# One order for all five queues of a transformer block, planned while it is traced

## The chip, the cores and the metric

The kernel runs on one core of a Trainium2 chip. The metric is the device time of one execution in microseconds; beside it there is the profile of one execution of the same program. The engines are called as in the profile: PE is TensorE (matrix products), PEld its weight loads, DVE is VectorE, ACT is ScalarE, POOL is GpSimd, and SP is the queue from which this kernel issues all its DMAs.

## The reference, cut to what matters

The input x has 8 batches of 1024 tokens with 512 features. After one layer norm, causal attention with 16 heads of 32 features and a feed-forward network with blockwise FP4 quantisation run side by side on the same normalised tokens, and both are added to x:

```python
xn = _layernorm(x, axis=-1)
x = x + _L0_attn_ref(xn, W_attn, b_attn, W_proj, b_proj) + _L0_ffn_ref(xn, w_gate, w_up, w_down)

def fp4_quant_dequant(x):           # along the last dim, blocks of 16
    scale = jnp.maximum(jnp.max(jnp.abs(xb), axis=-1, keepdims=True) / 6.0, 1e-12)
    xn = xb / scale
    idx = jnp.searchsorted(_MID, jnp.abs(xn))
    return _GRID[idx] * jnp.sign(xn) * scale

gate, y = fp4_linear(x, w_gate), fp4_linear(x, w_up)      # 512 -> 1408
h = jax.nn.silu(gate) * y
return fp4_linear(h, w_down)                              # 1408 -> 512
```

`fp4_linear` quantises both its operands, so the weights, the normalised tokens and the hidden values all go through the quantisation. Everything is in float32.

## The kernel before

**Tiles and units.** Tokens are worked on in 64 tiles of 128 (`Tile`, eight to a batch). Attention is worked on in 64 units (`Unit`): two heads of one batch over its 1024 tokens. Values that are needed later (q and k split into a high and a low part, v, quantised tokens, attention outputs, partial results) go to DRAM and come back.

**The pieces of work**, each a generator that traces instructions and yields a cost in microseconds of PE time:

- `prepare` (with `normed`, `keep_quantised`, `project`): a tile's layer norm (L265 to L269: statistics on DVE, one power on POOL, one scaling on DVE), its transposes on PE with a copy by ACT (L222, L223), its quantised form, and, for each second tile, the q, k and v projections (L322, L359). ACT moves q and k from PSUM to the one buffer `full` (L333), DVE splits them (L342, L343), SP stores them.
- `maxima`: for a unit, all scores are computed once (L414) for their row maxima: DVE adds the causal mask in PSUM (L422) and takes the maximum (L423), then makes a small table of statistics that PE transposes (L437), ACT copies (L439, `statT`) and SP sends through DRAM into `shT`.
- `weigh`: scores are computed a second time with the maxima subtracted by an extra matmul (L497, L500), ACT takes the exponential (L508), POOL zeroes the masked part (L511) and adds up the sums (L469, L472), PE multiplies by v (L479) and sums the sums (L537).
- `network`: gate and up products of a tile in pairs of column chunks (L611), silu by ACT (L623), product by DVE (L626), quantisation, transposes, the down product (L596), and a part result (L603) kept in DRAM.
- `finish`: the attention output of a tile is loaded (`yT`, L677), normalised by the inverse sums (L687, L688), projected (L696) and added to the part result (L701).
- `weights_quantised`: 34 pieces of the three FFN weight matrices are loaded, quantised and transposed into SBUF; the first half beside the first batch's `prepare`, the second half over the first eight units.
- `quantised`: the quantisation, ten instructions of DVE (L201 to L215). For weight pieces the two multiplies by a spread scale (L208, L215) run on POOL.

**What sets the order.** The outer loop runs over the units. In step n it merges the preparation of tile n+10, the finish of tile n-10, `weigh` of unit n, the network's next tile (from n = 8 on; before that weights and `prepare_late`), and `maxima` of unit n+1. `merge` always advances the stream with the smallest share of its total done. `passed` advances one clock by the cost said, and actions that were put off with `Later` (mostly DMA issues) are traced when the clock passes their time. PE, ACT and SP keep the order in which the instructions were traced (`manual_schedule`); the order on DVE and POOL is chosen by the framework's scheduler when the program is built.

**PSUM.** The pool `ps_g` has six banks used in turn under the name `g`; `y` and `acc` have one bank each.

## Time and profile before

| | |
|---|---|
| time, median of 3 runs | 4896.89 us (4888.65 to 4902.39) |
| the profiled execution's own time | 4902.55 us |
| span of its instructions | 4900.8 us |
| mean granted TensorE clock | 0.957 |
| busy PE / DVE / POOL / ACT | 91% / 62% / 37% / 29% |
| mean DMA rate over the span | 123 GB/s of HBM |

The span runs from the first to the last instruction of one execution. Lines such as L423 are lines of the kernel's source. A PE time is modelled at its end, so a busy PE is not PE at its peak. A float32 matmul appears as two records in the profile. "A <- B" in a list of waits says that B's end released A; the columns after it are the total in us, how often, and the longest.

### The profile page before, as it was taken

What the parts mean: (1) busy time and instruction counts of PE and PEld (TensorE: products, weight loads), DVE (VectorE), ACT (ScalarE), POOL (GpSimd) and SP (SyncE); (2) the same over time, 40 slices, a digit from 0 to 9 for tenths busy, and PEclk for the clock granted to TensorE, in tenths of its full rate; (3) what the DMA queues carried; (4) which work ended last, traced back from release to release, by engine and by line L of the source; (5) the groups of instructions that cost most, each with busy time, mean ns of one, the idle gap of its engine ahead of it and who ended that gap; (6) DMA issues with size and microseconds to landing.
All of it is one profiled execution on the core that took longest, in us unless ns stands there. A gap on an engine that the chain in (4) does not pass through costs nothing.

```text
span 4900.8 us, 59197 instructions
## 1 busy us (share of the span) xinstructions
PE 4482.6 (91%) x18708; PEld 2698.6 (55%) x18708; DVE 3060.8 (62%) x6903; ACT 1444.1 (29%) x2892; POOL 1836.1 (37%) x2652
## 2 busy tenths in 40 slices
PE   6567778999999999999999999999999999999999
PEld 5444445555555555555555555555555555555554
DVE  6577665656566665656666565666666566666555
ACT  1122223332323333332333333233233333333210
POOL 2145443433433343333343334334333334444300
PEclk9778889999999999999999999999999999999999
DMA  6544443444544453554445445444445444333221
GB/s 189 165 111 120 121 119 90 139 118 131 151 120 136 132 145 115 136 147 124 132 134 141 118 141 143 124 136 132 135 125 141 138 124 114 95 90 77 67 64 63
DMA packets 609145, 605.35 MB, mean 124 GB/s; under 512 B 133824, under 2 KB 464064, under 8 KB 608832
## 3 DMA queue, kind: packets, MB, share of 16 engines
q1 hardware_dynamic: 608832, 601.57, 43.9%
q8 instruction: 149, 2.44, 0.2%
q14 instruction: 164, 1.34, 0.1%
HBM read 431.50 MB, written 169.87 MB: 123 GB/s over the span
## 4 chain that ended last, share of the span: by engine, by line
PE 68%; DVE 16%; ACT 2%; DMA 2%; issue 2%; POOL 1%; SPq 1%; ACTq 0%; DVEq 0%; POOLq 0%
PE g L611 23%; PE acc L596 9%; PE g L322 7%; PE y L479 5%; PE g L696 4%; PE g L497 4%; PE g L414 4%; PE g L359 4%; PE g L500 4%; DVE neg L423 3%; PE g L222 2%; DVE scale L201 1%; PE g L537 1%; DVE inv L204 1%; DVE g L422 1%
## 5 line engine op out<-in xcount | busy, mean ns | idle before, releaser
L472 POOL TENSOR_TENSOR sum<-sum,pr 128x512 f32<-128x512 f32 (+3 forms) x1024 | 948.4, 935 | 605.8 <-ACT pr L508 560.7
L508 ACT ACTIVATE pr<-g 128x512 f32<-128x512 f32 (+3 forms) x1536 | 680.2, 494 | 1280.5 <-PE g L500 1265.5
L423 DVE TENSOR_REDUCE neg<-g 128x1 f32<-128x512 f32 (+3 forms) x1536 | 811.5, 548 | 79.3 <-PE g L414 69.1
L511 POOL TENSOR_SCALAR_AFFINE_SELECT pr<-pr 128x128 f32<-128x128 f32 x1024 | 361.6, 358 | 1136.7 <-ACT pr L508 1111.5
L414 PE MATMUL g<-ks,qs 128*128 128x512 f32 (+3 forms) x1536 | 694.6, 499 | 88.6 <-ACT full L333 43.6
L611 PE MATMUL g<-wuT,xqT_in 128*128 128x512 f32 (+1 forms) x1536 | 707.8, 591 | 47.7 <-DVE neg L423 47.7
L497 PE MATMUL g<-shT,pick 128*128 128x512 f32 (+3 forms) x1536 | 646.3, 429 | 83.6 <-DVE neg L423 64.9
L611 PE MATMUL g<-wgT,xqT_in 128*128 128x512 f32 (+1 forms) x1536 | 678.9, 568 | 1.7
L596 PE MATMUL acc<-wdT,hqT 128*128 128x512 f32 x1408 | 667.4, 595 | 1.4 <-ACT hqT L223 1.4
L422 DVE TENSOR_TENSOR g<-g,mask 128x128 f32<-128x128 f32 x1024 | 286.8, 291 | 557.8 <-PE g L414 555.0
L322 PE MATMUL g<-xnT,wa 128*128 128x256 f32 x2048 | 504.4, 403 | 42.4 <-ACT xnT L223 26.1
L500 PE MATMUL g<-qs,ks 128*128 128x512 f32 (+3 forms) x1536 | 534.0, 355 | 0.0
L469 POOL TENSOR_TENSOR sum<-pr 128x512 f32<-128x512 f32 x256 | 339.7, 1339 | 485.7 <-ACT pr L508 475.7
L322 PEld LDWEIGHTS g<-xnT,wa 128*128 128x128 f32 x2048 | 417.7, 206 | 120.1 <-ACT xnT L223 27.6
L414 PEld LDWEIGHTS g<-ks,qs 128*128 128x128 f32 x1536 | 285.4, 197 | 319.8 <-issue 114.7
L611 PEld LDWEIGHTS g<-wuT,xqT_in 128*128 128x128 f32 x1536 | 286.5, 196 | 316.1 <-issue 201.7
L479 PE MATMUL y<-pr,vs 128*32 128x512 f32 (+3 forms) x3072 | 431.2, 516 | 24.1 <-POOL pr L511 23.3
L497 PEld LDWEIGHTS g<-shT,pick 128*128 128x128 f32 x1536 | 298.9, 195 | 244.9 <-DVE neg L423 109.1
L611 PEld LDWEIGHTS g<-wgT,xqT_in 128*128 128x128 f32 x1536 | 280.8, 191 | 234.5 <-issue 169.4
L596 PEld LDWEIGHTS acc<-wdT,hqT 128*128 128x128 f32 x1408 | 259.6, 190 | 230.5 <-issue 209.9
L500 PEld LDWEIGHTS g<-qs,ks 128*128 128x128 f32 x1536 | 300.8, 196 | 76.7 <-issue 45.0
L333 ACT ACTIVATE full<-g,bqk 128x256 f32<-128x256 f32 x256 | 107.3, 470 | 626.0 <-PE g L322 307.7
(98 smaller groups left out, 4740.7 us busy)
## 6 DMA issues: line engine op xcount, KB each, us to landing
wa<-in_L_attn_W_attn_dram SPq DMA_DIRECT2D x192, 512.0 KB
qs<-qk_kept SPq DMA_DIRECT2D x512, 128.0 KB
ks<-qk_kept SPq DMA_DIRECT2D x512, 128.0 KB
wp<-in_L_attn_W_proj_dram SPq DMA_DIRECT2D x93, 512.0 KB
qk_kept<-high SPq DMA_DIRECT2D x128, 256.0 KB
qk_kept<-full SPq DMA_DIRECT2D x128, 256.0 KB
y_kept<-yu SPq DMA_DIRECT2D x256, 128.0 KB
yT<-y_kept SPq DMA_DIRECT2D x128, 256.0 KB
```

The costliest lines, as they stand in the source:

```text
L322: nc.tensor.matmul(pq[:, j, :], lhsT=wa[:, c, j * P : (j + 1) * P], rhs=xnT[:, c, :], start=(c == 0), stop=(c == NC - 1),)
L414: nc.tensor.matmul(sc[:, :n], lhsT=un.qs[Q][:, r, i * P : (i + 1) * P], rhs=un.ks[h][:, r, :n], start=True, stop=True,)
L423: nc.vector.tensor_reduce(neg[:, Q + h, k : k + 1], sc[:, :n], AX.X, ALU.max, negate=True)
L469: nc.gpsimd.tensor_tensor(sums[r], prs[0][0], prs[1][0], ALU.add)
L472: nc.gpsimd.tensor_tensor(sums[r][:, q0:], sums[r][:, q0:], pr[:, q0:], ALU.add)
L479: nc.tensor.matmul(y[row : row + HD, q0:], lhsT=un.vs[h][:, jj, r * HD : (r + 1) * HD], rhs=pr[:, q0:], start=(j < 2), stop=(j >= last - 1 ...
L497: nc.tensor.matmul(w[:, q0:], lhsT=pick[:, Q * HU + r, :], rhs=un.shT[:, q0:], start=True, stop=False)
L500: nc.tensor.matmul(w[:, q0:], lhsT=un.ks[h][:, r, jj * P : (jj + 1) * P], rhs=un.qs[Q][:, r, q0:], start=False, stop=True,)
L508: nc.scalar.activation(pr[:, q0:], w[:, q0:], AF.Exp)
L511: nc.gpsimd.affine_select(out=pr[:, q0 : q0 + P], in_=pr[:, q0 : q0 + P], compare_op=ALU.is_ge, fill=0.0, base=0, pattern=[[1, P]], channe ...
L596: nc.tensor.matmul(tl.acc, lhsT=job.hqT[:, j, :], rhs=wdT[:, i, :], start=(i == 0), stop=(i == NI - 1))
L611: nc.tensor.matmul(job.g[:, : job.w], lhsT=job.tl.xqT[:, c, :], rhs=wT[:, c, job.i0 : job.i0 + job.w], start=(c == 0), stop=(c == NC - 1),)
```

## The change

The kernel now keeps a clock for each engine besides the one for PE, and every piece of work says to them what it puts on ACT, DVE and POOL. A step yields up to four values: its PE cost, the time from which its inputs should be there, how many free PSUM banks it needs, and its weight in the sharing. `merge` takes, among the streams whose share is within 0.3 of the smallest, one that can start now; if none can, it lets the clock pass to the earliest. `passed` handles put-off actions in the order of their times. All five engines are in `manual_schedule`, so DVE and POOL too keep the traced order.

The six banks become six fixed tiles (`Banks`); a step takes the one that the clock says is free first. The quantisation becomes the class `Quantised`: seven steps, each put off to its own time, spaced at 1.4 times their length; at most two are under way, with two `step` buffers where there was one. Only the first 17 weight pieces use POOL for the multiplies. The layer norm yields between the power on POOL and the scaling on DVE. The split of q and k, the load of the part result and the inverse of the sums have times of their own; `yu` has one buffer where it had two.

The diff, cut to its core:

```diff
+    def on(engine, us, after=0.0):
+        free[engine] = max(free[engine], clock[0], after + HOP) + us
+        return free[engine]
+
+    def act(columns, after=0.0, function="other"):
+        ...
+        return on("act", 0.1 + 0.00095 * columns + switch, after)
...
     def passed(us):
-        clock[0] += us
-        for entry in [e for e in waiting_list if e.due <= clock[0]]:
-            waiting_list.remove(entry)
-            entry.now()
+        end = clock[0] + us
+        while True:
+            due = [e for e in waiting_list if e.due <= end]
+            if not due:
+                break
+            first = min(due, key=lambda e: e.due)
+            waiting_list.remove(first)
+            clock[0] = max(clock[0], first.due)
+            first.now()
+        clock[0] = end
+
+    class Banks:
+        def __init__(self):
+            self.tiles = [ps_g.tile([P, W], F32, name=f"bank{k}") for k in range(6)]
+            self.at = [0.0] * 6
+        def when(self, count):
+            return sorted(self.at)[count - 1] if count else 0.0
+        def take(self):
+            k = self.at.index(min(self.at))
+            self.at[k] = float("inf")
+            return k, self.tiles[k]
+        def back(self, k, time):
+            self.at[k] = time
...
-    def quantised(src, w, xs, spreader=None):
...
+    class Quantised:
+        def __init__(self, src, w, xs, after=0.0, helper=False):
+            while len(running) > 1:
+                running[0].done()
+            running.append(self)
+            ...
+            start = max(0.0, after - clock[0])
+            for wide, us, engine, action in self.operations(src, w, xs, helper):
+                us = us + wide * w / CW
+                self.left.append(Later(start, lambda us=us, engine=engine, action=action: self.one(us, engine, action)))
+                start += SPREAD * us
+            self.expected = clock[0] + start
...
-            done.append((piece, quantised(raw, piece[4], raw, nc.gpsimd)))
-            yield 0.0
...
+            done.append((piece, Quantised(raw, piece[4], raw, helper=k < EARLY)))
+            while len(done) > (1 if k + 1 < len(pieces) else 0):
+                (_, dst, r, c, w), wq = done.pop(0)
+                yield 0.0, wq.ready(), 1
+                transposed(dst[:, c // P : (c + w) // P, r : r + P], wq.done(), w // P)
+                if len(pieces) > k + 2:
+                    loaded.append(load(*pieces[k + 2]))
+                yield 0.11 * w / P, 0.0, 0, 0.5
...
         nc.gpsimd.tensor_tensor(rstd, rstd, power, ALU.pow)
+        yield 0.0, pool(0.6, dve(1.05)), 0
         nc.vector.tensor_scalar(xt, xt, mv[:, 0:1], rstd, ALU.subtract, ALU.mult)
+        tl.ready = dve(0.6)
...
-                nc.vector.tensor_copy(high, full)
-                nc.vector.tensor_tensor(low, full, high.bitcast(F32), ALU.subtract)
+                def split(full=full, high=high, low=low):
+                    nc.vector.tensor_copy(high, full)
+                    nc.vector.tensor_tensor(low, full, high.bitcast(F32), ALU.subtract)
+                    dve(1.1)
...
-                stored.append(Later(4.0, store))
-                yield 3.4
+                stored.append(Later(end - clock[0] - 0.3, split))
+                stored.append(Later(end - clock[0] + 2.0, store))
+                yield 3.44, 0.0, 1
...
                     nc.vector.tensor_reduce(neg[:, Q + h, k : k + 1], sc[:, :n], AX.X, ALU.max, negate=True)
-                    yield n * 0.00044
+                    end = dve(0.08 + 0.00105 * n, end)
+                    banks.back(bank, end)
+                    yield cost, 0.0, 1
...
                 if j % 2 == 0 and waiting:
-                    yield weighted()
+                    yield 2 * cost, max(ready, emptied), 0
+                    yield weighted(), 0.0, 2
                     waiting = []
...
-            yu = p2.tile([P, W], F32, name="yu")
+            yu = p1.tile([P, W], F32, name="yu")
...
+        part = load_part() if tl.part is not None else None
+        yield 0.0, clock[0] + 6.0, 0, 1.0
         nc.vector.tensor_tensor(yT, yT, more, ALU.add)
         nc.vector.tensor_tensor(yT, yT, inv, ALU.mult)
-        yield 3.0
-        part = load_part() if tl.part is not None else None
+        yield 0.0, dve(1.4), 1, 1.0
...
+    def merge(streams):
+        live = [Stream(total, steps) for total, steps in ((t, s) for s, t in streams)]
+        while live:
+            least = min(s.share() for s in live)
+            start = lambda s: max(s.ready, banks.when(s.banks))
+            near = [s for s in live if s.share() - least < AHEAD_OF_OTHERS] or live
+            now = [s for s in near if start(s) <= clock[0] + 0.05]
+            if now:
+                s = min(now, key=Stream.share)
+            else:
+                s = min(near, key=start)
+                ...
+                if start(s) > clock[0]:
+                    passed(start(s) - clock[0])
+            if not s.step():
+                live.remove(s)
...
-        engines={mybir.EngineType.PE, mybir.EngineType.Activation, mybir.EngineType.SP}
+        engines={
+            mybir.EngineType.PE,
+            mybir.EngineType.Activation,
+            mybir.EngineType.DVE,
+            mybir.EngineType.Pool,
+            mybir.EngineType.SP,
+        }
...
-                streams.append((maxima(units[n + 1]), 7.0))
+                streams.append((maxima(units[n + 1]), 6.0))
```

## The prediction

> **What bounds the kernel now.** I read the page first (engines, slices), then the busy table by stage, then the waits of TensorE in each stage, then one stall in the timeline. From the page:
>
> ```profile
> PE 4482.6 (91%) x18708; PEld 2698.6 (55%) x18708; DVE 3060.8 (62%) x6903; ACT 1444.1 (29%) x2892; POOL 1836.1 (37%) x2652
> PE   6567778999999999999999999999999999999999
> PEclk9778889999999999999999999999999999999999
> ```
>
> TensorE is the bound from slice 8 on. Before that neither it nor any other engine is full, and its granted clock is low. The transpose of the 64 units' statistics (statT, one per unit) marks the stages: units' statistics start at 229.1 us, the feed-forward network joins at about 737, token preparation ends at about 4030, the last unit's statistics are at 4553.3. The busy table over these stretches (columns: stretch, length, then busy us of PE, weight load, DVE, ACT, POOL; clock; DMA share; GB/s):
>
> ```profile
> 0.00:229.00 229.00, 148.77 (x617) 121.39 (x617) 137.04 (x316) 37.74 (x79) 50.39 (x64) 0.85 0.60 183
> 229.00:737.00 508.00, 344.37 (x1590) 223.42 (x1590) 341.22 (x762) 135.64 (x303) 243.71 (x339) 0.83 0.43 117
> 737.00:4030.00 3293.00, 3146.05 (x13287) 1893.23 (x13286) 2059.08 (x4702) 1043.34 (x2070) 1257.06 (x1839) 0.97 0.47 132
> 4030.00:4553.00 523.00, 505.69 (x2129) 280.55 (x2128) 340.81 (x759) 174.86 (x341) 238.96 (x350) 0.99 0.37 92
> 4553.00:4901.00 348.00, 337.69 (x1095) 179.99 (x1091) 182.68 (x365) 52.52 (x99) 45.97 (x62) 1.00 0.21 65
> ```
>
> TensorE stands idle for 80, 164, 147, 17 and 10 us: 418 us in all, which is what there is to win, and the cycles lost to a low clock after a stall. What ended the idle time, for TensorE in the second stage and then in the third:
>
> ```profile
> PE g L437 <- DVE stat L433: 44.3, 9, 10.1
> PE g L414 <- ACT full L333: 43.6, 4, 12.8
> PE y L479 <- POOL pr L511: 22.8, 27, 3.6
> PE g L222 <- POOL hid L215: 15.4, 1, 15.4
> ...
> PE g L497 <- DVE neg L423: 54.9, 48, 2.1
> PE g L611 <- DVE neg L423: 47.7, 23, 2.1
> PE g L414 <- DVE neg L423: 17.1, 45, 2.0
> PE g L414 <- ACT hid L623: 11.5, 22, 0.8
> ```
>
> In the third stage 119.7 of 147 us are matmuls that wait for a PSUM bank still held by an earlier score tile, because its row maximum (L423) has not been taken. DVE is only 63% busy there (2059 of 3293): it is not short of time, its queue is in the wrong order. One such stall, once per unit, in the timeline:
>
> ```profile
> 1996.47 0.15 DVE L267 TENSOR_SCALAR rstd<-mv 128x1 f32<-128x1 f32 x1
> 1996.70 0.55 POOL L268 TENSOR_TENSOR rstd<-rstd,power 128x1 f32<-128x1 f32 x1 [11.15 <-DVE rstd L267]
> 1997.28 0.55 DVE L269 TENSOR_SCALAR xt<-xt,mv,rstd 128x512 f32<-128x512 f32 x1 [0.66 <-POOL rstd L268]
> 1998.30 0.69 DVE L343 TENSOR_TENSOR full<-full,high 128x512 fp32r<-128x512 f32 x1
> 1998.91 0.29 DVE L422 TENSOR_TENSOR g<-g,mask 128x128 f32<-128x128 f32 x1
> 1999.72 0.70 PE L497 MATMUL g<-shT,pick 128*128 128x512 f32 x1 [2.11 <-DVE neg L423]
> 1999.80:2003.20 3.40, 3.40 (x9) 2.64 (x9) 1.06 (x2) 1.19 (x2) 1.59 (x2) 0.51 0.31 111
> ```
>
> The layer norm's chain stands as one block in DVE's queue, with a round trip to POOL inside it (0.66 us idle), and the split of q and k behind it. The maximum that frees the bank comes after both; TensorE waits 2.11 us. The last row is the busy table right after: the clock is 0.51 for 3.4 us, so the same matmuls take 1.7 us longer. A unit of the third stage takes 3293/46 = 71.6 us; 3.2 us of it are idle TensorE, 1.7 the slow window (47 such windows lie in the stage).
>
> **A rule against the row.** The Trainium skill, TensorE: Matmul & The Clock Gate, Part 1, puts the fall to half rate after at least one idle window of about 3.4 us[...]. By it a 2.11 us stall would cost no clock, and the third stage would hold 147 us to win. The rows show the slow window after a stall shorter than that, so I count 147 + 46 x 1.7 = 225 us.
>
> **The change, part by part.** The instructions are the same ones: in the built programs PE has 12366, ACT 2894 and SP 3854 in both; DVE goes from 6905 to 6939, POOL from 2657 to 2623.
>
> *The second 17 weight pieces stay on DVE.* 34 multiplies leave POOL (1117 and 1088 ns) for DVE (719 and 692 ns in the same shape): +24 us on DVE, nearly all in the second stage, 341 + 24 = 365 of 508 us, beside TensorE. It costs nothing while DVE has slack; if the stage shrinks under about 400 us it becomes the bound. Against it stands a rule: the skill's SBUF — State Buffer, Who interferes with whom, says a two-input DVE instruction contends with a POOL instruction that reads SBUF, through the shared port. The trace fits: the add L213 takes 662 ns on hid, 1120 on xs, where POOL's sums run. So the planner's 0.67 us is too short by up to 0.45 there; taking 34 reads of about 1.1 us off POOL gives back up to 37 us. Net between -13 and +24 on DVE, off the path; I take +24.
>
> *DVE and POOL in traced order.* DVE now keeps the order in which the program's own clock emits. In the order of before, 71 of 72 norm chains have no row maximum between L267 and L269; in the new one 14 of 72 have none, and from the fourth batch on each has three. The split of q and k is emitted when ACT should be done; a quantisation goes out as seven steps at 1.4 times their length instead of ten instructions at once. So the bank-freeing maxima pass between. What is gained is the stall above and its slow window. What is late next: the mask step on POOL (weight loads of the y matmuls already wait 0.41 us each for L511) and the silu bank (11.5 us above), so I do not take all of 225 us but 70%: **-158**. Bounds: -225, and upwards the rival below.
>
> *Waits moved into the order.* A TensorE step now goes in when its input should be there. The 15.4 us for a weight piece (L222 <- L215) is a transpose placed by share alone; so is the wait for statistics (44.3). Score maxima also end later in their unit (share total 6.0, was 7.0), which thins DVE's work before the statistics but leaves less cover for the shift's trip through DRAM (14 us of waits in this stage now). ACT's 43.6 us is a queue blocked by `full`, one buffer whose stores must land; stores are now due 2 us after ACT, still one buffer. Of 164 us idle I take half, **-80**: the stage then lasts 428 us, DVE at 365/428 = 85%. Bounds: 0, and -143 with DVE full.
>
> *The head (0 to 229).* `full`, the two W_attn buffers and 183 GB/s remain. What goes is a weight piece not ready (9.9) and a norm not ready (12.5): 22 us, I take **-20**; bounds 0 and -45.
>
> *DVE behind DMA.* DVE waited 303.6 us for yT in the third stage, 13.8 us each time, since its order put L687 before the load was issued. Now it is emitted 6 us after the issue; the trace shows about 5.5 from issue to start. TensorE's waits name none of this, so it is worth 0 to a few us, inside the 158.
>
> *Six fixed banks, two step buffers, one yu buffer.* Six banks as before; now the one free earliest is taken: 0, bounds +-1 us a unit. A second step buffer lets two quantisations overlap: 0 or less. One yu instead of two: the y copies are at least 18 us apart and their stores go within a few us: 0.
>
> *DMA order.* Same transfers. Weight loads start after the transpose that frees their buffer (three up front); the part load comes 6 us earlier; the inverse goes out 8 us after its load, was 12. SP has 3854 entries either way, and these pass only single loads: 0.
>
> *Last stages.* 17 us idle and three slow windows in the fourth: **-10**. The fifth is dense: **-2**.
>
> Sum: -20 - 80 - 158 - 10 - 2 = -270. The profiled execution took 4902.55 us (span 4900.8), 5.7 over the median of 4896.89: 4632 against it, 4627 against the median. Predicted: 4630.
>
> **The rivals.**
>
> *Half of it.* Only one of the two stages gives: the second stays near 508 because DMA trips and `full` bound it, or the third keeps its stall because real durations drift from the planned ones. 4897 - 80..190: 4710 to 4815. For: ACT's and the shift's waits are DMA latencies that no order shortens.
>
> *Nearly all of it.* 225 + 143 + 45 + 20 = 433: 4465. Against: a plan in round numbers, with contention left out.
>
> *Slower: DVE's FIFO blocks in new places.* The plan charges no contention and fixed DMA times; an instruction placed too early holds every maximum behind it, TensorE stalls about 2.1 us and then runs 1.7 us of lost clock: 3.8 us. The second stage still gives 80 and the head 20. One stall more than now in each of 56 units costs 213, so 4897 - 100 + 213 = 5010. It decides from 26 extra stalls, about one in every second unit. Against: in before's queue, chosen by a scheduler with costs of its own, this is what already happens once a unit; the new order holds at most some 4 us of DVE work between maxima in a steady unit, with six banks of slack.
>
> *It does not do what it says.* The built order shows all five queues as traced; 2% at most.
>
> **How the numbers follow.** The forecast 0.57 (own range 4550 to 4715); half 0.18; nearly all 0.07; no effect 0.03; slower 0.15. I take 4490 to 4890: under it some 0.05, over it 0.15. Within 0.3% (about what measurement here can tell): 0.04. Faster 0.81, slower 0.15.
>
> **What would show it.** In the profile after: a third stage of about 68 us a unit, no 2 us wait for the row maximum, few slow windows, PE about 98% busy there; a second stage near 430 us with DVE at 85%; no DVE wait for yT over 3 us. Wrong if the maxima's waits stay, or TensorE's new waits are for the mask step or quantised pieces, or the second stage stays above 480.

## The result and the profile after

The changed kernel takes 4872.0 us (median; 4862.8 to 4880.2) against 4895.0 us of the kernel before on the same chip: ratio 0.9952, interval 0.9936 to 0.9968. It is faster by 0.5%, where 5.5% had been forecast. The profiled execution took 4870.0 us (span 4868.3).

The page after, engines, TensorE's busy slices and granted clock, and the chain of work that ended last:

```profile
PE 4445.5 (91%) x18708; PEld 2643.2 (54%) x18708; DVE 3326.0 (68%) x6937; ACT 1459.5 (30%) x2892; POOL 1847.5 (38%) x2618
PE   6577779999999999999999999999999999999998
PEclk8778889999999999999999999999999999999999
PE 53%; DVE 25%; DMA 11%; POOL 3%; SPq 3%; issue 2%; ACT 1%; ACTq 0%; DVEq 0%; POOLq 0%
```

TensorE's idle time is 423 us, as it was (418): the change won no idle time at all. What it won is 37 us of busy TensorE. By stage (table below) that is 68 us less in the third and 36 more in the second (where 49 more matmul records now fall). In the third the clock is better: its records hold 24 half-speed windows (92 us at a granted clock of 0.50) instead of 47 (167 us), which is worth half of the 75 us, 37. Where the other 31 us of that stage come from was not followed. DVE is busy 265 us longer for 24 us of added work. The chain that ended last runs through DVE and DMA for 36%, where it was 18% (DVE 16%, DMA 2%).

The busy table over the same stages (stretch, length, busy us of PE, weight load, DVE, ACT, POOL; clock; DMA share; GB/s):

```profile
0.00:241.40 241.40, 149.33 (x621) 120.38 (x621) 144.04 (x310) 39.25 (x81) 49.77 (x61) 0.82 0.58 177
241.40:758.50 517.10, 379.97 (x1639) 234.54 (x1639) 386.66 (x794) 139.35 (x310) 227.28 (x312) 0.81 0.42 115
758.50:3985.00 3226.50, 3077.88 (x13277) 1839.90 (x13277) 2262.79 (x4715) 1055.07 (x2069) 1277.35 (x1839) 0.99 0.48 134
3985.00:4504.10 519.10, 501.84 (x2111) 272.73 (x2110) 353.52 (x754) 177.72 (x346) 244.39 (x349) 0.99 0.35 91
4504.10:4868.30 364.20, 336.49 (x1066) 175.67 (x1064) 178.96 (x364) 48.12 (x92) 48.69 (x60) 0.99 0.21 62
```

The head went from 229 to 241 us, the second stage from 508 to 517, the third from 3292.5 to 3226.5 (boundaries to a tenth, 70.1 us a unit), the fourth from 523.7 to 519.1, the last from 347.5 to 364.2. The forecast had 209, 428, 3135, 513 and 346. Waits of TensorE in the third stage, then in the last (engine, line, what ended the wait: us in all, times, longest):

```profile
PE bank L627 <- DVE neg L545: 49.4, 22, 3.4
PE bank L861 <- DVE neg L545: 29.0, 20, 1.6
PE bank L535 <- DVE neg L545: 23.9, 36, 2.0
PE bank L561 <- DVE stat L557: 15.9, 24, 2.1
...
PE bank L323 <- DVE hid L316: 19.9, 11, 2.7
```

In the last stage transposes wait 19.9 us for a quantisation's last step (L316). In the third the row maximum (L545) still holds the banks, for 102 us in the first three rows against 119.7 us in the three such rows before. What holds DVE is new: beside its waits for TensorE's scores, which it had before too, its list of waits has one that was not there:

```profile
DVE z L715 <- DMA z<-sums_kept: 120.8, 24, 6.3
```

One such stall in SP's timeline (start, length, the issues):

```profile
2317.72 2.29 SPq L504 DMA_DIRECT2D qs<-qk_kept  x4
2320.05 3.52 SPq L504 DMA_DIRECT2D ks<-qk_kept  x4
2323.65 2.13 SPq L504 DMA_DIRECT2D qs<-qk_kept  x4
2325.89 2.13 SPq L504 DMA_DIRECT2D ks<-qk_kept  x4
2328.13 1.12 SPq L516 DMA_DIRECT2D vs<-v_kept  x2
2329.29 0.50 SPq L713 DMA_DIRECT2D z<-sums_kept  x1
```

The same moment in DVE's timeline, and then in TensorE's; in brackets the idle time before, and what ended it:

```profile
2327.37 0.69 DVE L853 TENSOR_TENSOR yT<-yT,inv_y 128x512 f32<-128x512 f32 x1
2332.66 0.25 DVE L715 RECIPROCAL z<-z 128x16 f32<-128x16 f32 x1 [4.61 <-DMA z<-sums_kept]
2332.83 0.63 DVE L545 TENSOR_REDUCE neg<-bank 128x1 f32<-128x512 f32 x1
```
```profile
2333.52 0.50 PE L627 MATMUL bank<-shT,pick 128*128 128x512 f32 x1 [1.79 <-DVE neg L545]
```

The load of the softmax sums (L713) is planned 8 us after their store, its reciprocal 5 us later. On SP the load stands behind 18 issues for the next unit (the halves of q and k, and v), which take 11.5 us (2317.72 to 2329.25), and the plan charges SP nothing. So DVE reaches a 0.25 us reciprocal whose data are not there and stands for 4.61 us with every row maximum behind it. In the stage's 46 units the load stands behind such a burst 23 times, and DVE stalls in all 23; of the other 23 it stalls in one. What follows the stall on TensorE, in the busy table:

```profile
2335.00:2338.40 3.40, 3.40 (x7) 1.96 (x6) 3.30 (x8) 0.00 (x1) 0.00 (x0) 0.50 0.42 128
```

The granted clock is 0.50 for 3.4 us again.

### The profile page after: what moved, and what is told of

It reads as the page before. It is cut to its first block, busy times and chain, and to the rows that moved or that the text cites. A ratio compares the mean times of both kernels' runs of the same rounds, so it can differ in the third digit from the quotient of the medians.

```text
span 4868.3 us, 59460 instructions
## 1 busy us (share of the span) xinstructions
PE 4445.5 (91%) x18708; PEld 2643.2 (54%) x18708; DVE 3326.0 (68%) x6937; ACT 1459.5 (30%) x2892; POOL 1847.5 (38%) x2618
## 3 DMA queue, kind: packets, MB, share of 16 engines
q1 hardware_dynamic: 608832, 601.57, 44.3%
## 4 chain that ended last, share of the span: by engine, by line
PE 53%; DVE 25%; DMA 11%; POOL 3%; SPq 3%; issue 2%; ACT 1%; ACTq 0%; DVEq 0%; POOLq 0%
PE bank L768 16%; PE acc L748 9%; DVE neg L545 4%; PE bank L432 4%; PE y L609 4%; PE bank L627 3%; PE bank L535 3%; PE bank L630 3%; PE bank L861 3%; PE bank L476 3%; DMA qs<-qk_kept 3%; PE bank L323 2%; DMA z<-sums_kept 2%; POOL sum L603 2%; DMA ks<-qk_kept 2%
## 5 line engine op out<-in xcount | busy, mean ns | idle before, releaser
L603 POOL TENSOR_TENSOR sum<-sum,pr 128x512 f32<-128x512 f32 (+3 forms) x1024 | 988.8, 976 | 749.3 <-ACT pr L638 714.2
L638 ACT ACTIVATE pr<-bank 128x512 f32<-128x512 f32 (+3 forms) x1536 | 679.5, 491 | 1070.2 <-PE bank L630 859.7
L545 DVE TENSOR_REDUCE neg<-bank 128x1 f32<-128x512 f32 (+3 forms) x1536 | 840.6, 555 | 173.6 <-PE bank L535 138.0
L535 PE MATMUL bank<-ks,qs 128*128 128x512 f32 (+3 forms) x1536 | 659.8, 472 | 85.8 <-DVE neg L545 46.1
L627 PE MATMUL bank<-shT,pick 128*128 128x512 f32 (+3 forms) x1536 | 653.4, 433 | 56.4 <-DVE neg L545 56.0
L768 PE MATMUL bank<-wgT,xqT_in 128*128 128x512 f32 (+1 forms) x1536 | 688.6, 578 | 3.8 <-ACT hqT L324 0.7
L768 PE MATMUL bank<-wuT,xqT_in 128*128 128x512 f32 (+1 forms) x1536 | 680.3, 574 | 2.2 <-ACT pr L638 2.1
L630 PE MATMUL bank<-qs,ks 128*128 128x512 f32 (+3 forms) x1536 | 531.4, 354 | 0.0
L598 POOL TENSOR_TENSOR sum<-pr 128x512 f32<-128x512 f32 x256 | 350.0, 1391 | 359.4 <-ACT pr L638 359.4
L432 PE MATMUL bank<-xnT,wa 128*128 128x256 f32 x2048 | 475.9, 387 | 3.2 <-DMA wa<-in_L_attn_W_attn_dram 1.4
L432 PEld LDWEIGHTS bank<-xnT,wa 128*128 128x128 f32 x2048 | 394.6, 195 | 81.4 <-issue 20.8
L627 PEld LDWEIGHTS bank<-shT,pick 128*128 128x128 f32 x1536 | 301.9, 197 | 228.0 <-DVE neg L545 90.1
```

What stands on the lines that cost most here:

```text
L432: nc.tensor.matmul(pq[:, j, :], lhsT=wa[:, c, j * P : (j + 1) * P], rhs=xnT[:, c, :], start=(c == 0), stop=(c == NC - 1),)
L535: nc.tensor.matmul(sc[:, :n], lhsT=un.qs[Q][:, r, i * P : (i + 1) * P], rhs=un.ks[h][:, r, :n], start=True, stop=True,)
L545: nc.vector.tensor_reduce(neg[:, Q + h, k : k + 1], sc[:, :n], AX.X, ALU.max, negate=True)
L598: nc.gpsimd.tensor_tensor(sums[r], prs[0][0], prs[1][0], ALU.add)
L603: nc.gpsimd.tensor_tensor(sums[r][:, q0:], sums[r][:, q0:], pr[:, q0:], ALU.add)
L627: nc.tensor.matmul(w[:, q0:], lhsT=pick[:, Q * HU + r, :], rhs=un.shT[:, q0:], start=True, stop=False)
```

## The experiments

Three theories. *Queue*: single instructions, put into an in-order queue before their input is there, block what frees the banks. *Bank*: the order is right, but six banks do not cover DVE's real durations. *Contention*: DVE runs 265 us longer because POOL's additions now lie beside other DVE work. Edits are to the changed kernel ("after") unless another is named; each run's ratio is to the kernel before on the same chip.

### Where the third stage went

**The later inverse.**
```
-            Later(5.0, lambda: nc.vector.reciprocal(z, z))
-            Later(8.0, lambda: nc.sync.dma_start(out=inverses, in_=z))
+            Later(14.0, lambda: nc.vector.reciprocal(z, z))
+            Later(17.0, lambda: nc.sync.dma_start(out=inverses, in_=z))
```


> The reciprocal of a unit's sums is put 14 us after its load (was 5), the store of the inverses 17 us after it (was 8). Queue theory (in an in-order DVE each wait that the plan has too short becomes a TensorE stall plus a slow clock window; the load of the sums stands behind some 20 other issues on SP): the 24 DVE waits of about 5 us for the sums go, with a TensorE stall of about 2 us and 1.7 us of slow clock each: 24 x 3.8 = about 90 us, so 4780 to 4800. Bank theory (the stalls come from six banks and TensorE's own order, whatever DVE's order): within 15 us of 4872. Contention theory (POOL's sums stretch two-input DVE instructions and so delay the row maxima): 4850 to 4872.

Measured 4785.1 us, ratio 0.9778 (0.9763 to 0.9793). The third stage:

```profile
755.80:3904.40 3148.60, 3050.26 (x13277) 1842.26 (x13276) 2284.49 (x4715) 1051.07 (x2069) 1277.54 (x1839) 0.99 0.50 138
```

Six banks, TensorE's order and the DVE work are the same, so the bank theory, which had the time within 15 us of 4872, falls.

**The load ahead of the halves.** After itself, with only SP's order changed; DVE, ACT, PE and POOL issue in the order of after.
```
-                    Later(8.0, invert)
+                    Later(1.5, invert)
-            Later(5.0, lambda: nc.vector.reciprocal(z, z))
-            Later(8.0, lambda: nc.sync.dma_start(out=inverses, in_=z))
+            Later(11.5, lambda: nc.vector.reciprocal(z, z))
+            Later(14.5, lambda: nc.sync.dma_start(out=inverses, in_=z))
```


> After itself, with the load of a unit's sums put 6.5 us earlier in SP's order, ahead of the 18 issues that load the next unit's halves and values; the reciprocal and the inverse's store stay where they were, and the orders of DVE, ACT, PE and POOL are those of after. If the load is late because of SP's queue, DVE's wait for z (120.8 us in 24 waits in the third stage) goes nearly all, and the time is that of the later reciprocal: 4780 to 4795. If it is the trip itself that is long (the sums' stores must land first, and SP then waits for them with 18 loads behind it), the wait stays at half or more and the halves come late too: 4850 to 4900.

Measured 4757.2 us, ratio 0.9710 (0.9697 to 0.9723), better than expected. The third stage in the busy table:

```profile
761.80:3875.80 3114.00, 3033.59 (x13277) 1827.89 (x13277) 2264.53 (x4715) 1051.73 (x2069) 1283.52 (x1839) 1.00 0.50 139
```

DVE's wait for z there, and TensorE's largest wait:

```profile
DVE z L715 <- DMA z<-sums_kept: 4.9, 2, 2.5
...
PE bank L861 <- DVE neg L545: 23.2, 22, 1.1
```

Moving one load in SP's queue takes z's wait from 120.8 to 4.9 us, the stage from 3226.5 to 3114.0 (67.7 us a unit), its idle time from 149 to 80 us and its half-speed windows from 24 to 5. That is 112.5 us over 24 stalls, 4.7 us each. The loads that stood behind the 18 issues now stand ahead of them. In the other units the load now stands right behind such a burst, and DVE waits there in only one of 23, since the reciprocal follows 11.5 us after the planned load instead of 5. So the cause is the delay in SP's queue, which the plan did not charge; DVE's order, contention included, was otherwise good enough for the third stage that had been forecast. Why the later inverse keeps stalls of 2.1 us at L861 where these are 1.05 was not pursued.

**The kernel before, with its DVE and POOL in traced order** (its ACT, PE and SP orders unchanged):
```
         engines={ ...
+            mybir.EngineType.DVE,
+            mybir.EngineType.Pool,
```


> The kernel before with nothing changed but DVE and POOL put in traced order, so that each quantisation stands as ten instructions in one block, the layer norm with its trip to POOL in another, and loads and their users next to each other. Queue theory: clearly slower than 4895, by 3% or more (over 5040), since row maxima wait behind whole blocks and behind loads. Bank theory: within 1% of 4895.

Measured 5413.6 us, ratio 1.1061 (1.1043 to 1.1079). DVE's waits in its third stage:

```profile
DVE yT L687 <- DMA yT<-y_kept: 302.5, 22, 16.6
...
DVE high L342 <- ACT full L333: 239.0, 47, 6.2
DVE z L572 <- DMA z<-sums_kept: 179.5, 46, 7.5
```

Traced order without planned times costs 10.6%; TensorE's waits for the row maximum at L497 and L414 go from 72.0 to 242.6 us in that stage. Of the three waits shown the first stood in before as well (303.6 us), the second was 35.9 us, and the third is new. The change's clock removes the first two (7.5 us are left for the split, none for yT) and a third of the last.

**After, with DVE and POOL left to the scheduler.** The reverse: the two lines above taken out of after.

> The changed kernel with DVE and POOL taken out of the fixed order again, so the framework's scheduler orders them; TensorE, ACT and SP keep the planned order. Queue theory: the planned DVE order is worth something against the scheduler's, except for the sums' wait; without it 4900 to 4990. Bank theory: DVE's order does not matter, 4860 to 4885. Contention theory: near 4872, DVE busy still well above 3061 us if POOL's work falls at the same times.

Measured 4920.9 us, ratio 1.0059 (1.0041 to 1.0077). With the planned order the third stage is shorter (3226.5 against 3336.7) and the fourth (519 against 535). But of TensorE's 236 us of idle time in this run's third stage most is one wait for the projection's weights, which after does not have:

```profile
PE bank L861 <- DMA wp<-in_L_attn_W_proj_dram: 146.7, 22, 8.0
```

SP keeps its planned order here while DVE no longer keeps its own, so this run does not show that DVE's planned order alone is the better one there. The planned order is worse in the head (241 against 231), the last stage (364 against 342), and above all the second:

```profile
231.40:704.20 472.80, 352.14 (x1639) 224.27 (x1639) 345.28 (x788) 138.77 (x311) 224.23 (x317) 0.86 0.47 126
```

With the same matmuls the scheduler does the second stage in 472.8 us, the plan in 517.1.

### Contention

**After without the 1024 POOL additions into the sums (L603),** the plan still charging them; the output lacks those terms.
```
-                            nc.gpsimd.tensor_tensor(sums[r][:, q0:], sums[r][:, q0:], pr[:, q0:], ALU.add)
```


> The changed kernel without 1024 of POOL's additions for the softmax sums (only the first two score tiles of each half are summed), the plan still charging them, so that all other instructions keep their order; the output's normalisation is not the reference's. POOL loses about 990 us of work. Contention theory: DVE's busy time falls by 150 us or more from 3326 and the time by 100 us or more (under 4770). Queue theory: DVE's busy time falls, but the sums' wait and the order's gaps stay: 4820 to 4850. Bank theory: 4860 to 4872.

Measured 4792.7 us, ratio 0.9790 (0.9773 to 0.9808). DVE's wait for z stays at 121.7 us, and DVE is busy 3055.7 us instead of 3326.0: 270 us of DVE's time give 79 us, less than the 100 that the contention theory had asked for. The kernel before was not run without its additions, so how much of the 79 us it loses too is not known.

**Both: the later inverse, and no additions.**

> The later inverse without the 1024 later POOL additions into the sums (the output then lacks those terms of the softmax's sum). Alone, the one gave 87 us and the other 79. If the stall behind z and the contention are two separate losses, the gains add: 4872 - 87 - 79 = about 4706, third stage near 67.5 a unit. If contention only costs where DVE already holds the banks because of the z step, they overlap and the time stays above 4745.

Measured 4671.6 us, ratio 0.9535 (0.9517 to 0.9552): 4.2% under after, where the single gains are 1.7% and 1.6%. They are two separate losses. The third stage of this run, and then DVE's groups in the third stage of before (L433), after (L557, L297) and this run (L557, L297; here from 755.8 to 3904.4 us, some 105 us into the next stage), with busy us and mean ns:

```profile
724.30:3799.70 3075.40, 3017.05 (x13277) 1823.85 (x13276) 2073.41 (x4715) 1042.87 (x2069) 593.98 (x1103) 1.00 0.51 141
```

```profile
L433 DVE TENSOR_TENSOR stat<-neg,stat 128x8 f32<-128x8 f32 x92 | 36.2, 433 | 0.0
```
```profile
L557 DVE TENSOR_TENSOR stat<-neg,stat 128x8 f32<-128x8 f32 x92 | 91.8, 998 | 3.2
L297 DVE TENSOR_SCALAR step<-hid 128x512 int32<-128x512 int32 x138 | 86.4, 626 | 2.4
```
```profile
L297 DVE TENSOR_SCALAR step<-hid 128x512 int32<-128x512 int32 x141 | 56.5, 400 | 2.5
L557 DVE TENSOR_TENSOR stat<-neg,stat 128x8 f32<-128x8 f32 x94 | 15.8, 169 | 3.2
```

A subtraction of eight columns (L557) takes 169 ns without the additions and 998 ns on average in after. There 89 of its 92 instances overlap one of POOL's additions in the trace and take 1026 ns; the other three take 168. In before it was 24 long ones of 92. This agrees with the Trainium skill, SBUF — State Buffer, Who interferes with whom, by which a DVE instruction with two inputs in SBUF contends with a POOL instruction that reads SBUF, and tensor_scalar forms can. The subtraction and the multiply on hid (L315, L316) went from 652 and 645 ns to 763 and 807, and stay at 755 and 804 in this run. Its trace shows why: 22 of 138 are long (1402 and 1672 ns, the others about 635), and all but one of the 44 long ones overlap the first addition of each sum (L598), which this run keeps.

### Second stage and head

In the second stage of the later inverse, what TensorE waits for most, and then one stretch of POOL's timeline there:

```profile
PE y L609 <- POOL pr L644: 39.8, 18, 5.2
```
```profile
397.89 0.55 POOL L373 TENSOR_TENSOR rstd<-rstd,power 128x1 f32<-128x1 f32 x1 [14.69 <-DVE rstd L372]
398.40 1.94 POOL L644 TENSOR_SCALAR_AFFINE_SELECT pr<-pr 128x128 f32<-128x128 f32 x3
```

The layer norm's power, one column, stands in POOL's queue 14.7 us before its input is there, with the masks behind it: the same fault as z, on POOL.

**The power 6 us later** (from the second batch on, and in the feed-forward part's norms):
```
+        if wait:
+            yield 0.0, dve(1.05) + wait, 0
+            nc.gpsimd.tensor_tensor(rstd, rstd, power, ALU.pow)
+            yield 0.0, pool(0.6), 0
+        else:
             nc.gpsimd.tensor_tensor(rstd, rstd, power, ALU.pow)
             yield 0.0, pool(0.6, dve(1.05)), 0
...
-            yield from normed(tiles[tl.n + 1])
+            yield from normed(tiles[tl.n + 1], 6.0 if tl.n >= NT else 0.0)
...
-        yield from normed(tl)
+        yield from normed(tl, 6.0)
```


> The later inverse with the layer norm's power (POOL, L373) traced 6 us after the statistics from the second batch on and for the tiles that the feed-forward part prepares, and the normalisation after it. Queue theory: in the second stage POOL stands 171.5 us in 15 waits for DVE's L372 (35.5 us before), since DVE runs behind its plan, and the masks and sums behind it make the y matmuls (39.8 us) and the z matmuls (17.0 us) wait; with the power later at least half of those 57 us go and the second stage falls from 514 to about 485, the third by 0 to 20: about 4750. Contention theory: the y and z matmuls wait because the sums run 1.0 us each and not because they start late; the stage stays within 5 us of 514: 4780 or more.

Measured 4851.2 us, ratio 0.9914 (0.9899 to 0.9928). TensorE's waits in its second stage (five lines were added ahead of these):

```profile
PE bank L323 <- DVE res L316: 49.1, 8, 9.6
...
PE y L614 <- POOL pr L649: 8.8, 10, 1.1
```

The wait for masks goes from 39.8 to 8.8 us, so that wait is explained. But DVE now waits 31.4 us for the power, and TensorE waits 49.1 us for late quantisations; the stage is 522 us instead of 514. The wait moved on. Most of the 66 us lost against the later inverse lie elsewhere: the third stage goes from 3148.6 to 3204.1 us, where TensorE's largest wait is a bank that ACT empties into `full` (18.3 us with the later inverse):

```profile
PE bank L632 <- ACT full L448: 72.1, 22, 3.4
```

The next two runs meet the same wait. This edit was not tried again with that wait gone.

**Split and stores of q and k 2 us later.**
```
-                stored.append(Later(end - clock[0] - 0.3, split))
-                stored.append(Later(end - clock[0] + 2.0, store))
+                stored.append(Later(end - clock[0] + 1.7, split))
+                stored.append(Later(end - clock[0] + 4.0, store))
```


> The later inverse with the split of q and k, and its stores, traced 2 us later. Queue theory: in the head DVE stands 59.8 us at the split for ACT's bias step, which itself runs behind the plan since the projection's matmuls run at the low clock; weight pieces' quantisations stand behind it, and TensorE waits 41.7 us for those. With the split 2 us later some 15 to 30 us of DVE's wait go and the head falls from 242 to about 230; the second stage gains a few us for the same reason: about 4770. Rival: the head is held by the transfers (183 GB/s there), DVE's wait is only where it shows, and with full in one buffer a later split delays the next bias step: head 242 or more, 4785 to 4800.

Measured 4979.3 us, ratio 1.0168 (1.0149 to 1.0187), outside both expectations. ACT's waits in the third stage have the reason:

```profile
ACT full L443 <- DMA qk_kept<-full: 227.9, 23, 11.1
```

`full` has one buffer. A store 2 us later makes ACT's next bias step wait for it (118.4 us with the later inverse), and TensorE waits 78.5 us for a bank that ACT should empty.

**DVE's planned durations times 1.15,** with the later inverse.
```
-        return on("dve", us, after)
+        return on("dve", 1.15 * us, after)
...
-            self.end = on(engine, us, self.end)
+            self.end = on(engine, us * (1.15 if engine == "dve" else 1.0), self.end)
```

> The later inverse, with every duration that the plan charges to DVE multiplied by 1.15 (DVE is busy 3326 us where the same kernel without the POOL additions needs 3056, so contention stretches it by 9%, and the small steps by more). Contention theory: the plan's waits come from durations too short; with longer ones the quantised pieces and banks are expected later, TensorE does other work first, and the stall for statistics, banks and quantised pieces fall: 4740 to 4765. Queue theory: what is late is late by DMA trips and by other engines, not by DVE's own length, and 15% moves nothing in the order that matters: 4775 to 4795, either sign.

Measured 4951.3 us, ratio 1.0104 (1.0087 to 1.0121). TensorE's largest wait of the third stage is again the bank behind `full`:

```profile
PE bank L677 <- ACT full L443: 84.2, 22, 5.2
```

**`full` in two buffers** (zs in one instead of two, for room), with the later inverse.
```
-                full = p1.tile([P, 2, QW], F32, name="full")
+                full = p2.tile([P, 2, QW], F32, name="full")
... (the two other tiles of that name, for v and for a constant, likewise)
-            zs = p2.tile([P, W // 2], F32, name="zs")
+            zs = p1.tile([P, W // 2], F32, name="zs")
```


> The later inverse with two buffers for full (the projection's output before its split and store); zs has one buffer instead of two to make the room. Queue theory, in its form after the split put 2 us later cost 190 us: ACT stands 118 us in the third stage for the store that reads full, and TensorE's score matmuls wait 18.3 us for a bank that ACT should have emptied; in the second stage ACT stands another 39 us at full. With two buffers those go: the third stage falls from 68.5 to about 67.8 a unit, the second by 10 to 25 us, the head by up to 10: about 4730. Rival: the store is in time in most groups, ACT has slack (30% busy), and the waits are taken over by the row maxima: 4775 to 4795.

Measured 4770.3 us, ratio 0.9734 (0.9717 to 0.9752): 12 us less in the head (242.1 to 229.8), 15 in the third stage, 7 more in the second (520 us). By the two ratios that is 22 us of the 55 expected.

**The two misses again, with `full` in two buffers.**

> Split and stores of q and k 2 us later, as in the run that lost 190 us, but with full in two buffers. If the single buffer was the trap (ACT's bias step waits for the store of the group before, and the banks with it), nearly all of the loss goes: 4765 to 4800, and no wait of TensorE for ACT's full in the third stage. If the later split itself costs (it meets other row maxima, and high still has one buffer), the loss stays for the larger part: 4870 to 4980.

> DVE's planned durations times 1.15, with full in two buffers (with one: 4951 us, 84 us of waits for ACT's full in the third stage). Trap: most of the loss goes, about 4780 to 4810, and what is left is the price or gain of the durations themselves. Else: the plan is worse by itself with longer durations, the statistics' wait (55 us) and the maxima stay, 4850 to 4950.

The later split: 4837.7 us, ratio 0.9889 (0.9870 to 0.9907); the longer durations: 4755.0 us, ratio 0.9719 (0.9698 to 0.9741). Against the same kernel without the edit, the two cost 194 and 166 us with one buffer; with two the first costs 67 and the second gives 15. So the single buffer was the whole loss of the longer durations, and most of that of the later split; what is left of that one shows as 51.7 us of TensorE waiting for statistics (15.9 without it) and 27.2 us of DVE waiting for the store of `high`, another single buffer. The 15 us are not clear of the noise by themselves, since the intervals of 0.9719 and 0.9734 overlap: the third stage gains 32 us (3133.4 to 3101.2), and the others lose 21 of them again. In the last run below the gain is clear.

**The plan's TensorE steps at 1.22 times their length until the feed-forward part joins,** with `full` in two buffers.
```
-            passed(cost)
+            passed(cost * pace[0])    # 1.22, and 1.0 from the ninth unit on
```


> With full in two buffers, the plan's clock moves on 1.22 times as far for each TensorE step until the feed-forward part joins (the granted clock is 0.81 to 0.82 there, 1/0.82 = 1.22). If the second stage is long because the plan runs ahead of a slow TensorE, inputs are now expected in the right order and it falls from 520 to 480 to 500, the head by 0 to 10: 4730 to 4755. If it is held by DMA trips and POOL's queue, order does little: 510 to 525, 4765 to 4780.

Measured 4779.6 us, ratio 0.9771 (0.9753 to 0.9790), second stage 531.8 us. So correcting the plan for the slow TensorE by this one factor does not shorten the stage.

**All 34 weight pieces' multiplies on POOL again,** with the later inverse.
```
-            done.append((piece, Quantised(raw, piece[4], raw, helper=k < EARLY)))
+            done.append((piece, Quantised(raw, piece[4], raw, helper=True)))
```


> The later inverse with all 34 weight pieces' two multiplies on POOL again instead of the first 17 pieces: 34 multiplies leave DVE (24 us) for POOL (37 us). If DVE's time in the second stage is what holds it (387 of 517 us busy), it falls by 10 to 20 us: 4765 to 4775. If POOL's queue is (its masks and sums stand behind late inputs), 34 more instructions that wait for DVE in POOL's queue make it longer by 10 to 40 us: 4795 to 4825. The forecast's term for this edit was +24 us off the path, that is nothing: 4785.

Measured 4801.2 us, ratio 0.9810 (0.9796 to 0.9825), second stage 524.7 us against 513.7. DVE is busy 28 us less, POOL 24 us more. That part of the change is worth 11 us in the stage and 16 in all. POOL now waits 90 us for DVE in front of these multiplies (50.7 and 39.7), and TensorE 44.3 us for masks instead of 39.8; this fits what was expected of POOL's queue, though the 11 us were not followed wait by wait.

### The last stage

**A quantisation's steps 1.0 times their length apart instead of 1.4,** with the later inverse, and then with `full` in two buffers.
```
-    SPREAD = 1.4
+    SPREAD = 1.0
```


> The later inverse (4785 us) with a quantisation's seven steps traced at 1.0 times their planned length one after another instead of 1.4. Queue theory: in the tail nothing else fills DVE, so the spread only delays the last step; the turn transposes wait for it there (19.9 us, L323 <- L316) and the tail should go from 364 to about 345; elsewhere a step that goes out too close to its predecessor blocks nothing, as it is on the same engine. About 4765. Contention theory: the quantisation's steps are long because POOL reads at the same time; the spread is not what costs, and the tail stays at 360 or more: 4785. Against both: denser steps hold the row maxima in the third stage back by up to a step and a half (1.2 us) per quantisation; if that counts, the third stage goes from 68.5 back to 69.5 a unit and the time to 4820.

> As with two buffers for full, and a quantisation's steps traced 1.0 times their length apart instead of 1.4. With one buffer the denser steps gave 15 us in the third stage (4 slow windows instead of 17) and 16 in the tail, and took 14 in the head and 23 in the fourth stage. If the losses came from ACT's steps at full (the head's ACT waits), two buffers take them back and the gains add: about 4710. If they came from row maxima and statistics standing behind seven dense steps, they stay: 4735 to 4750.

Measured 4790.9 us, ratio 0.9788 (0.9774 to 0.9803), and 4772.3 us, ratio 0.9740 (0.9725 to 0.9754). Both times the last stage falls to 348 us and the fourth rises from about 520 to 541; the third has 4 and 3 half-speed windows. In the head the first run loses 13.6 us, the second 3.6. Denser steps gain in the last stage, where DVE has nothing else. In the fourth TensorE's waits for statistics and maxima go from 13.1 to 26.1 us in the first of the two runs, some half of what is lost there.

**Steps at 1.0 after the last unit only,** with `full` in two buffers.
```
-                start += SPREAD * us
+                start += spread[0] * us    # SPREAD, and 1.0 after the last unit
```

> With full in two buffers, and the steps of a quantisation at 1.0 times their length only after the last unit. If the tail's loss is the spread alone, it falls from 366 to 349 as it did with 1.0 everywhere, and nothing else moves: 4753. If the 17 us there came from what the earlier stages left behind, the tail stays at 360 or more: 4766 to 4772.

Measured 4748.6 us, ratio 0.9707 (0.9684 to 0.9730); the last stage 348.1 us instead of 366.0, the others as they were. So the last stage's loss is the spread.

**What gained, together:** later inverse, `full` in two buffers, DVE's durations times 1.15, steps at 1.0 after the last unit.

> Later inverse, full in two buffers, DVE's planned durations times 1.15, and the quantisation's steps at 1.0 times their length after the last unit. If the gains add: 4755 - 27 (the tail from 377 to 350) = 4728. If the longer durations undo the tail's gain: 4750.

Measured 4724.0 us, ratio 0.9641 (0.9628 to 0.9654): the fastest version with the whole computation, 3.6% under before and 3.1% under after. Against the run before this one (ratio 0.9707) it has only the longer durations more, so these gain 0.7%. Its third and last stages:

```profile
756.00:3857.20 3101.20, 3015.76 (x13277) 1829.12 (x13276) 2300.24 (x4715) 1054.20 (x2069) 1282.70 (x1842) 1.00 0.51 140
4376.20:4718.30 342.10, 331.44 (x1058) 175.72 (x1056) 182.78 (x364) 47.91 (x91) 46.19 (x58) 1.00 0.22 66
```

The load put ahead of the halves was not tried in this combination.

## Why the prediction was wrong

- **The sign was right, the size was not:** -270 us was the sum, -23 the result, and -33 between the two profiled executions. Two stages gained 71 us and three lost 38, so the sign was a narrow thing. Of the 237 us missing, 92 lie in the third stage, 89 in the second, 32 in the head, 19 in the last and 5 in the fourth.
- **The step that failed in the third stage: "DMA order", counted as 0,** since the moved transfers "pass only single loads". The inverse's load did not pass anything; it stood behind 18 issues, and DVE's reciprocal was tied to its planned time. It cost 112.5 us. The step compared the order of the transfers and did not ask which instruction of an in-order engine now waits for each.
- **The third stage, -158:** measured -66 with that stall, and -178.5 with only that load moved (3292.5 to 3114.0). The reading was right: the stall behind norm and split, the half-speed window after it, and the share of 70% was on the low side (178.5 of 225 is 79%). The sum lacked the new stall.
- **The slower rival had the mechanism,** "an instruction placed too early holds every maximum behind it", and about its price: 3.8 us a stall forecast, 4.7 measured. It happened in 24 units, near the 26 from which it was to decide. It was weighed as a matter of chance, though in SP's order the load stands behind 18 others in every second unit.
- **The step that failed in the second stage: "Of 164 us idle I take half", -80;** measured +9. Half was a share of the whole, not a sum over the waits named. The wait for a weight piece is gone and that for statistics is 9.6 us instead of 44.3, but masks behind POOL's early power wait 38.7 us instead of 22.8, and taking those away brought late quantisations (49.1 us). DVE is 75% busy there, and the stage is 32 us shorter without POOL's additions (517 to 485). The scheduler's order of DVE and POOL does 472.8 us, so at least 44 us are a matter of order; which instructions have to move stays open.
- **The head, -20:** measured +12; two buffers for `full` give those 12 back. The prediction named `full` with its one buffer, and then did not charge it.
- **The last stage, -2:** measured +17, all from the 1.4 spread, which the sum did not cost at all. The fourth, -10: measured -5.
- **Weight pieces on DVE, +24 us off the path:** the size was right (28 us), and the path gains 11 to 16.
- **"DVE behind DMA", yT's wait to vanish:** right; it is not in the stage's list any more. z took its place.
- **"The plan charges no contention"** was said in two rivals and given no size: without the additions after is 79 us shorter, the later inverse 114.
- **Its own signs of being wrong came true:** the maxima's waits stay (102 us), new waits are for the mask step, and the second stage stays above 480.
- **The rule against the row:** the row held. A stall of 1.79 us was still followed by a half-speed window; where the stalls at L861 had shrunk to 1.1 us, after the load was moved, the windows were nearly gone as well (47, 24, 5). The traces say more than the prediction used. The clock's records change only on a grid of 3.41 us, and a fall goes with how long TensorE was busy in the stretch before. In the traces of before, after and the run with the load moved, a full-rate stretch with TensorE busy for under 40% of it was followed by one at half rate in all 143 cases, one with 60% or more in none of 3682, and those between in 40 of 83. The stall of 1.79 us fell into one stretch (2331.6 to 2335.0) and left TensorE busy for 1.61 us of it, 47%; one of 1.1 us takes a third of a stretch at most. This is a count over the records; no run varied the stall alone.

## What to carry to other kernels

When all queues are in traced order, list for each instruction of an in-order engine the transfer that it waits for, and count the issues ahead of that transfer on its own queue; a plan that charges issues nothing is late by their sum. A stall has to be followed through every queue to its next owner, since moving one instruction often only passes the wait on. Look for single buffers between an engine and a store before tuning the order: with one, a shift of 2 us in the plan cost 194 us here, with two 67.

## What the runs showed that was not expected

- An eight-column subtraction on DVE takes 168 ns by itself and 1026 ns where one of POOL's additions lies beside it. Those additions take 970 ns on average in that stage, so a small instruction can take as long as the POOL instruction that it meets.
- The two losses (the stall behind z, POOL's additions) taken away together gave 4.2%, more than the 3.4% of their sum. The clock accounts for that: in the third stage TensorE is at half rate for 92 us in after, 65 with the later inverse and 126 without the additions, but for 20 us with both. If the changes added up it would be 99; half of the difference is 39 us, and the surplus is 34.
- SP's 18 issues took 11.5 us, 0.64 us each; the load that stood behind them took 3.4 us from issue to use.
